# More picked columns on ScalarE, and a new place for the transposes and for the norm's products in a message-passing kernel

## The chip, the cores and the metric

The kernel runs on one core of one Trainium2 chip. The metric is the device time of one execution in microseconds (us); before the change the median of three runs is 3556.44 us. The engines are named as in the profile: PE is TensorE (PEld its weight loads), DVE is VectorE, ACT is ScalarE, POOL is GpSimd, SP issues DMAs; a small q behind a name means the engine's sequencer, which waits and issues.

## The reference

A graph network's layer with 12500 nodes of 128 features (32 scalars and 32 vectors of 3), and 412500 edges that are sorted by the node they point to (`dst`). Each edge has 4 attributes and 8 radial inputs. A residual and a layer norm follow.

```
x0 = x[:, :32];  x1 = x[:, 32:].reshape(N, 32, 3)
feat0, self0 = split(x0 @ W1_0e / sqrt(32));  feat1, self1 = split(einsum('nui,uw->nwi', x1, W1_1o) / sqrt(32))
e0 = feat0[src];  e1 = feat1[src]                        # one row of 128 numbers for each edge
h  = gelu(edge_attr_8 @ W_mlp1 / sqrt(8));  h = gelu(h @ W_mlp2 / sqrt(64))      # 64 wide
w00, w01, w10, w11 = h @ Wp_00, h @ Wp_01, h @ Wp_10, h @ Wp_11                  # 32 wide each
mid0 = [w00 * e0 * ea0,  w11 * sum(e1 * ea1) / sqrt(3)] / sqrt(2)
mid1 = [(w01 * e0) x ea1,  w10 * e1 * ea0] / sqrt(2)
n0, n1 = segment_sum(mid0, dst), segment_sum(mid1, dst)  # over sqrt(32)
y = cos(pi/8) * self + sin(pi/8) * [n0 @ W2_0e, n1 @ W2_1o] / sqrt(64)
out = layernorm(x + y)
```

## The kernel before

**Units of work.** A *run* is 512 edges in 4 columns of 128 (`Q` = 4); there are 806 runs (`NS`). A *chunk* is 4 runs; there are 202 (`NCH`). The main loop has one step per run, `s`; `c` is its chunk and `k` = 0 to 3 its place in the chunk. The order on PE, ACT, DVE and SP is the order in which the code is written; POOL takes its gathers as their operands allow.

**Source rows.** Every edge needs the feature row of its source node, tile `G[s]` of 128 x 4 x 128, in 19 buffers (`LEAD`). `gather(s + 18)` issues one indirect DMA on POOL for each column of the run (L222). The first 18 runs gather from `x` and are multiplied by the weights afterwards (`turn_rows`, `features`); the others gather from a table of features that the prologue computes and stores to memory. Three kinds of column aren't gathered. In every 14th run SP loads one column's 128 rows by single-row DMAs from the table (`aid`, L209). And DVE and ACT each *pick* the nodes of one column out of the transposed input `xT`, which lies in SBUF: each picked node is one copy of a 128 x 1 column to the tile `gt` (L190 on DVE, L192 on ACT), at an address that a register holds. When 128 are together, `picked_rows` multiplies them with the weights (PE, L198), and ACT copies the result into `G` (L199). `SLOTS` says how many columns an engine picks in a run, and in how many register loads (`pick_nodes`) and groups of copies (`pick`): 32 a run on average on DVE, 28 on ACT as 12 and 16. Thus one whole column in every 4 runs is DVE's, and one in every 4.57 runs is ACT's.

**The small network.** In step k = 1 `mlp1` computes the first layer of chunk c + 2 (PE L536, gelu on ACT L540), in step k = 3 `mlp2` the second (PE L551, ACT L556). `radial` turns a chunk's 8 inputs by a PE transpose (L527) and a copy on ACT (L529), for chunk c + 2 in step k = 0. `load_edges` brings them by a DMA from SP four chunks ahead, in step k = 3 (L496). `weights` makes the four products `w` (PE L569). The tiles in PSUM named `h`, which all of these use, have two buffers.

**Messages and sums.** DVE multiplies `w` with `G` to messages `M` in three parts (L637 once, L641 twice a run). `segments` sums them by PE into a window of nodes in PSUM (L666, L668), at places that `tile_places` has computed from the edges' first nodes (`tile_first`, 202 rows of 16 numbers in two tiles). After a chunk DVE adds the window to `acc` (L681).

**Norm.** Nodes are finished in 25 groups of 512. When a group's sums are complete, `norm` runs in the step k = 3 of the chunk after: `moments` multiplies the sums by the output weights (PE L698, L701) and copies the result (ACT L706), `move_sums` moves the rest of `acc` (ACT L428), and DVE clears the free part in quarters, one in each following step k = 1 (L425). `norm_on` (statistics and roots, one step k = 1 later) and `norm_end` (k = 2, scaling on ACT L742, stores from SP L260) follow.

**Other moved parts.** `turn_attributes` turns the 4 attributes of 32 runs (PE L521, ACT L523) and `load_indices` the indices of 128 runs (PE L468).

Of the kernel before, what the change touches and what calls it, by code (L numbers as in the profile page):

```python
# [21 lines left out]
P = 128  # L22
# [3 lines left out]
Q = 4  # L26
# [21 lines left out]
AID_FROM = 22  # L48
AID_LEAD = 16
STEPS = 12  # L50
SLOTS = {DVE: [(12, 12, 0), (12, 12, 8), (12, 12, 8), (12, 12, 16)], ACT: [(12, 16)]}
COL_Q = {DVE: Q - 2, ACT: Q - 3}
COL_FROM = {DVE: 12, ACT: 12}
LNB = 2
TURN_AT = (7, 9, 11, 13, 15, 17, 18, 20, 22, 24)


@with_exitstack
def gnn_kernel(ctx: ExitStack, tc: tile.TileContext, x, src, dst, ea4, ea8, w1_0, w1_1, wm1, wm2,
# [276 lines left out]

    def weight_loads():

        yield w1r, sub(wm1, 0, [[0, P // RAD], [HID, RAD], [1, HID]])
        yield w2b, sub(wm2, 0, [[0, 2], [HID, HID], [1, HID]])  # L340
        for j, w in enumerate((wp00, wp01, wp10, wp11)):
            yield wpb[:, j * MUL:(j + 1) * MUL], sub(w, 0, [[0, 2], [MUL, HID], [1, MUL]])
        for t, w in ((w20, w2_0), (w21, w2_1)):
            yield t[:MUL, :], w[:MUL, :]
            yield t[MUL:, :], sub(w, MUL * MUL, [[0, 3], [MUL, MUL], [1, MUL]])
        yield first_node, sub(dst, 0, [[1, 1], [CH * SB, NCH]])
        for b, t in enumerate(tile_first):
            c0, n = b * P, t.shape[0]
            last = c0 + n == NCH and E < NCH * CH * SB
            if last:  # L350
                yield (t[n - 1:n, :].rearrange("a (k o) -> a k o", o=1),
                       sub(dst, (NCH - 1) * CH * SB, [[1, 1], [0, CH * Q], [1, 1]]))
                k = -(-(E - (NCH - 1) * CH * SB) // P)
                yield t[n - 1:n, :k], sub(dst, (NCH - 1) * CH * SB, [[k * P, 1], [P, k]])
            yield t[:n - last], sub(dst, c0 * CH * SB, [[CH * SB, n - last], [P, CH * Q]])

    def make_w1b():

# [34 lines left out]
    NT = -(-NCH // P)  # L393
    tile_first = [cst.tile([min(P, NCH - b * P), CH * Q], I32, name=f"tf{b}") for b in range(NT)]

    def find_first():

        floor, strays = line(1), line(2)
        steps = [(0, 0)] + [(c + 1, (bs[-1] + 1) * GN) for c, bs in due.items() if c + 1 < NCH]
        for (r, n0), (z, _) in zip(steps, steps[1:] + [(NCH, 0)]):  # L400
            nc.vector.memset(floor[:, r:z], float(n0))
        nc.vector.tensor_tensor(floor, first_node, floor, op=OP.subtract)
        nc.vector.tensor_scalar(strays, floor, 0.0, float(ACC - SPAN), op0=OP.max, op1=OP.min)
        nc.vector.tensor_copy(first_at, strays)
        nc.vector.tensor_tensor(strays, strays, floor, op=OP.not_equal)
        nc.vector.tensor_reduce(odd[0:1, 2 * NB:2 * NB + 1], strays, axis=mybir.AxisListType.X, op=OP.add)

    def tile_places():

        for b, t in enumerate(tile_first):  # L410
# [233 lines left out]

    def places(c):

        b, r = divmod(c, P)
# [34 lines left out]


    pend, done = [], []
    before_last = due[NCH - 1][0] - 1

    def moments(b, sums=None):
        n0, nn, full, tail, tiles = group(b)
        if not pend:
            Y["y"] = wk.tile([P, LNB, XB, P], F32, name="y", bufs=1)  # L690
            Y["v"] = wk.tile([P, LNB * XB, 2], F32, name="mv")
            nc.vector.memset(Y["v"], 1.0)
        j = len(pend)
        pend.append(b)
        pt = ps.tile([P, XB, P], F32, name="h")
        at = n0 - base[-1] if b in due[NCH - 1] else 0
        for t, k in tiles:
            nc.tensor.matmul(pt[:k, t, :], xT[:, n0 + t * P:n0 + t * P + k], ws, start=True, stop=sums is not None)  # L698
            if sums is None:
                for a in range(4):  # L700
                    nc.tensor.matmul(pt[:k, t, :], A["now"][:, a, at + t * P:at + t * P + k], wpost[:, a, :],  # L701
                                     start=False, stop=a == 3)
            else:
                nc.vector.tensor_tensor(pt[:k, t, :], pt[:k, t, :], sums[:k, t, :], op=OP.add)
        if full:
            nc.scalar.activation(Y["y"][:, j, :full, :], pt[:, :full, :], AF.Copy)  # L706
        if tail:
            nc.scalar.activation(Y["y"][:tail, j, full, :], pt[:tail, full, :], AF.Copy)

    def statistics(b):  # L710
        j = pend.index(b)
        st = wk.tile([P, XB, 6], F32, name="bst")
        for t, k in group(b)[4]:
            nc.vector.bn_stats(st[:k, t, :], Y["y"][:k, j, t, :])
            nc.vector.bn_aggr(Y["v"][:k, j * XB + t, :], st[:k, t, :])

    def deviations():
# [5 lines left out]
    def normalise(last=False, keep=False):  # L723
# [9 lines left out]
        for j, b in enumerate(pend):  # L733
            if b in done:
                continue
            for t, k in group(b)[4]:
                i = j * XB + t - i0
                if last and t % 2:
                    nc.vector.tensor_scalar(y[:k, j, t, :], y[:k, j, t, :], r[:k, i:i + 1], m[:k, i:i + 1],
                                            op0=OP.mult, op1=OP.add)  # L740
                    continue
                nc.scalar.activation(y[:k, j, t, :], y[:k, j, t, :], AF.Identity,  # L742
                                     bias=m[:k, i:i + 1], scale=r[:k, i:i + 1])
            store_nodes(nc.sync, out, b, y[:, j])
        done[:] = pend if keep else []
        if not keep:
            pend.clear()

    def norm(bs):
        for b in bs:  # L750
            moments(b)
            move_sums()
            new_sums()

# [11 lines left out]
    def norm_last(bs):  # L766
# [6 lines left out]
        if len(pend) > len(done):  # L773
            deviations()
            normalise(True)

    odd_f = cst.tile([1, 1], F32)
    odd_i = cst.tile([1, 1], I32)
# [117 lines left out]
    with tc.manual_schedule(engines={PE, ACT, DVE, SP}):  # L896
# [7 lines left out]
        for b in range(min(AHEAD, NG)):  # L904
# [9 lines left out]
                 NG // 2 + 9: tile_places, NG // 2 + 10: lambda: mlp2(1), NG // 2 + 11: make_ws, NG: make_wpost}  # L914
        for b in range(NG + 2):
            if b < NG:
                turn(b)
# [28 lines left out]
        for s in range(NCH * CH + CH):  # L946
# [56 lines left out]
            if k < 3 and s < NS:  # L1003
                pick_nodes(DVE, s, 2)
                pick(DVE, P)
            if k == 1 and 1 < c < NCH:
                norm_on(due.get(c - 2, []))
            if k == 2 and 1 < c < NCH - 1:
                norm_end(due.get(c - 2, []))
            if k == 0 and c == NCH:  # L1010
                norm_end(due.get(c - 3, []))
                norm_on(due.get(c - 2, []))
                norm_end(due.get(c - 2, []))
# [53 lines left out]
```

## Time and profile before

| | us |
|---|---|
| median of 3 runs | 3556.44 (3555.64 to 3560.35) |
| the profiled execution | 3556.29 |
| its span, from first to last instruction | 3554.4 |
| PE busy | 3159.9 |
| DVE busy | 3129.2 |
| ACT busy | 2797.6 |
| POOL busy | 2667.6 |

Busy time is that of instructions in the engine; what a sequencer does, such as loading registers or issuing DMAs, isn't in it. In a row of the groups stands: line, engine, operation, output <- inputs, shapes, count, then busy us and mean ns of one, and after the second bar the engine's idle time just before them with what ended it. In a row of waits stands who waited for whom: us in total, times, longest. In a row of the timeline stands the start and the length in us, and in brackets the idle time before. In a row by windows stands the stretch, its length, and then the busy time and count.

### The profile page before, as it was taken

What the parts mean: (1) busy time and instruction counts of PE and PEld (TensorE: products, weight loads), DVE (VectorE), ACT (ScalarE), POOL (GpSimd) and SP (SyncE); (2) the same over time, 40 slices, a digit from 0 to 9 for tenths busy, and PEclk for the clock granted to TensorE, in tenths of its full rate; (3) what the DMA queues carried; (4) which work ended last, traced back from release to release, by engine and by line L of the source; (5) the groups of instructions that cost most, each with busy time, mean ns of one, the idle gap of its engine ahead of it and who ended that gap; (6) DMA issues with size and microseconds to landing.
All of it is one profiled execution on the core that took longest, in us unless ns stands there. A gap on an engine that the chain in (4) does not pass through costs nothing. (4 is left out here: it accounts for less than half of the span.)

```text
span 3554.4 us, 143693 instructions
## 1 busy us (share of the span) xinstructions
PE 3159.9 (89%) x28598; PEld 2755.6 (78%) x28598; DVE 3129.2 (88%) x29317; ACT 2797.6 (79%) x23671; POOL 2667.6 (75%) x2804
## 2 busy tenths in 40 slices
PE   6899898998898988998899898898899989888888
PEld 6777777787777777877788787787787777777777
DVE  2699999999999999999899899888899888889897
ACT  3488788788888888887887888877787887788785
POOL 7777777777777777777777777777777777777775
PEclk8999999998999999899998899989899999999998
DMA  8322332223322223322323323323323232232221
GB/s 199 70 62 68 63 64 65 63 61 74 64 60 67 63 60 74 64 60 62 68 61 70 67 59 64 65 63 68 65 62 64 59 69 63 60 69 63 60 65 47
DMA packets 579225, 239.29 MB, mean 67 GB/s; under 512 B 483651, under 2 KB 528747, under 8 KB 578347
## 3 DMA queue, kind: packets, MB, share of 16 engines
q0 software_dynamic: 89536, 183.55, 20.3%
q1 hardware_dynamic: 468041, 40.02, 9.1%
q10 hardware_dynamic: 20770, 6.47, 0.8%
q8 instruction: 252, 4.13, 0.5%
q14 instruction: 626, 5.13, 0.5%
HBM read 217.00 MB, written 12.80 MB: 65 GB/s over the span
## 5 line engine op out<-in xcount | busy, mean ns | idle before, releaser
L222 POOL DMA_INDIRECT G<-table,idx x2726 | 2598.9, 953 | 836.7 <-issue 718.5
L192 ACT ACTIVATE gt<-xT 128x1 f32 x22016 | 2166.7, 190 | 73.3 <-issue 53.6
L190 DVE COPY gt<-xT 128x1 f32 x25216 | 1728.6, 144 | 212.1 <-issue 172.9
L666 PE MATMUL sums<-own,M 128*128 128x96 f32 x6446 | 1354.8, 294 | 74.3 <-DVE M L641 73.0
L668 PE MATMUL sums<-own,M 128*128 128x96 f32 x6446 | 1319.7, 288 | 85.1 <-DVE M L641 84.1
L666 PEld LDWEIGHTS sums<-own,M 128*128 128x128 f32 x6446 | 1037.5, 201 | 181.9 <-DVE M L641 101.7
L668 PEld LDWEIGHTS sums<-own,M 128*128 128x128 f32 x6446 | 1035.3, 202 | 108.9 <-DVE M L641 107.6
L641 DVE TENSOR_TENSOR M<-w,G 128x384 f32<-128x384 f32 x1612 | 880.1, 547 | 0.0
L569 PE MATMUL w<-wpb,h 64*128 64x128 f32 x6448 | 649.3, 305 | 57.8 <-DVE M L641 56.3
L569 PEld LDWEIGHTS w<-wpb,h 64*128 64x128 f32 x6448 | 496.5, 197 | 199.6 <-issue 74.3
L637 DVE TENSOR_TENSOR M<-w,G 128x256 f32<-128x256 f32 x806 | 333.4, 414 | 34.4 <-issue 19.9
L540 ACT ACTIVATE h<-h 128x512 f32<-128x512 f32 x404 | 216.3, 586 | 178.6 <-PE h L536 165.7
L536 PE MATMUL h<-eT,w1b 64*128 64x128 f32 x3232 | 288.7, 319 | 8.4 <-ACT e L523 8.3
L536 PEld LDWEIGHTS h<-eT,w1b 64*128 64x128 f32 x3232 | 241.3, 218 | 38.7 <-ACT e L523 13.7
L556 ACT ACTIVATE h<-h 128x512 f32<-128x512 f32 x404 | 213.5, 577 | 26.3 <-PE h L551 22.5
L551 PE MATMUL h<-h,w2b 64*64 64x256 f32 x3232 | 222.6, 391 | 0.0
L199 ACT ACTIVATE G<-h 128x128 f32<-128x128 f32 x369 | 96.4, 277 | 120.5 <-PE h L198 76.4
L198 PE MATMUL h<-wf,gt 128*128 128x128 f32 x738 | 143.5, 294 | 1.9 <-ACT h L556 0.9
L529 ACT ACTIVATE eT<-h 128x128 f32<-128x128 f32 x202 | 56.0, 277 | 112.7 <-PE h L527 89.5
L551 PEld LDWEIGHTS h<-h,w2b 64*64 64x64 f32 x3232 | 104.5, 133 | 44.8 <-issue 0.5
L630 DVE TENSOR_TENSOR own<-oh,e 128x512 f32<-128x512 f32 x202 | 137.6, 681 | 0.7 <-issue 0.2
L681 DVE TENSOR_TENSOR acc<-sums,acc 128x384 f32 x202 | 111.2, 550 | 9.7 <-issue 6.2
(113 smaller groups left out, 1329.1 us busy)
## 6 DMA issues: line engine op xcount, KB each, us to landing
G<-table SPq DMA_DIRECT2D x7168, 0.5 KB
G<-table,idx POOLq DMA_INDIRECT x2726
e<-in_edge_attr SPq DMA_DIRECT2D x201, 64.0 KB
own<-in_x SPq DMA_DIRECT2D x24, 256.0 KB
table<-acc ACTq DMA_DIRECT2D x24, 256.0 KB
xt<-in_edge_attr SPq DMA_DIRECT2D x24, 256.0 KB
out<-y SPq DMA_DIRECT2D x24, 256.0 KB
xt<-in_dst SPq DMA_DIRECT2D x5, 256.0 KB
```

The lines of the kernel that those rows point to most:

```text
L190: nc.vector.tensor_copy(to, col)
L192: nc.scalar.activation(to, col, AF.Copy)
L222: nc.gpsimd.indirect_dma_start(out=G[s][:, q, :], out_offset=None, in_=x if s < raw_runs else table, in_offset=bass.IndirectOffsetOnAxis(a ...
L536: nc.tensor.matmul(p1[h][:, j // 2, j % 2, :], w1b[rows, j, :], eT[c][rows, :], start=True, stop=True)
L540: nc.scalar.activation(H1[c][h], p1[h].rearrange("p k j e -> p (k j e)"), AF.Gelu_apprx_tanh, scale=1.0 / math.sqrt(RAD))
L551: nc.tensor.matmul(p2[r][k * HID:(k + 1) * HID, h * n:(h + 1) * n], w2b[rows, :], H1[c][h][rows, k * n:(k + 1) * n], start=True, stop=True)
L556: nc.scalar.activation(H2[c][r].rearrange("p k j e -> p (k j e)"), p2[r], AF.Gelu_apprx_tanh, scale=1.0 / math.sqrt(HID))
L569: nc.tensor.matmul(WP[i][:, q, :], H2[c][q % 2][rows, k, q // 2, :], wpb[rows, :], start=True, stop=True)
L637: nc.vector.tensor_tensor(M[s][:, :, :, :MUL], w[:, :, :2 * MUL].rearrange("p q (a u) -> p q a u", a=2), g[:, :, None, :MUL].to_broadcast( ...
L641: nc.vector.tensor_tensor(M[s][:, :, j, MUL:].rearrange("p q (i u) -> p q i u", i=3), w[:, :, None, (2 + j) * MUL:(3 + j) * MUL].to_broadc ...
L666: nc.tensor.matmul(flat[:, bass.ds(at, 4 * FIRST_HALF)].bitcast(F32), M[s][:, q, 0, :], own[:, 3 * WIDE:], start=False, stop=False)
L668: nc.tensor.matmul(sb[:, 1:, bass.ds(at, 4 * WIDE)].bitcast(F32), M[s][:, q, 1, :], own[:, :3 * WIDE].rearrange("p (a j) -> p a j", a=3), ...
```

## The change

- `SLOTS` of ACT becomes (12, 8, 12): 32 columns a run in three register loads, with a `pick` in every step and a third `pick_nodes` behind it. The loads of the picked nodes' numbers follow from the numbers in `SLOTS`.
- `radial` moves from k = 0 (for chunk c + 2) to k = 2 (for chunk c + 3); `turn_attributes` from step 21 of 32 to step 24, `load_indices` from step 64 of 128 to step 66.
- `norm` is split: `norm_products` in the step k = 0 of the second chunk after the group's last, `norm_keep` (copy, move of the sums, start of the clearing) in k = 1, `norm_on` and `norm_end` at k = 2 and k = 0 after it.
- The group before the last makes the products of three of its four tiles in earlier chunks (`part`); for that `find_first` counts an edge that would still touch those tiles as odd, which leads to a general path. The last group is normalised from PSUM, and each of its tiles is stored by its own DMA, in turn from SP and ACT.
- The table of first nodes comes as tiles of 16, 128 and 58 rows; the first is loaded first in the prologue, the others after the loads of picked nodes, and `tile_places` treats them in step 9.

```diff
-SLOTS = {DVE: [(12, 12, 0), (12, 12, 8), (12, 12, 8), (12, 12, 16)], ACT: [(12, 16)]}
+SLOTS = {DVE: [(12, 12, 0), (12, 12, 8), (12, 12, 8), (12, 12, 16)], ACT: [(12, 8, 12)]}
...
+FIRST_TILES = 16
...
     def weight_loads():
 
+        yield from tile_loads(0)
         yield w1r, sub(wm1, 0, [[0, P // RAD], [HID, RAD], [1, HID]])
...
+    tile_from = [0, *range(FIRST_TILES, NCH, P)]
...
+        for t, (a, z) in enumerate(zip(done_at, done_at[1:])):
+            nc.vector.tensor_scalar(strays[:, a + 1:z + 1], strays[:, a + 1:z + 1], float((t + 1) * P), None, op0=OP.max)
...
-    def moments(b, sums=None):
+    def moments(b, sums=None, part=None, hold=False):
         n0, nn, full, tail, tiles = group(b)
+        if part is not None:
+            tiles = tiles[part:part + 1]
...
+        if sums is None and b == NG - 1:
+            Y["pt"] = pt
+            return
+        if part is not None:
+            nc.scalar.activation(Y["y"][:, j, part, :], pt[:, part, :], AF.Copy)
+            return
+        if hold:
+            Y["held"] = Y["y"][:, j], pt
+            return
...
+                if last:
+                    eng = nc.sync if t % 2 else nc.scalar
+                    eng.dma_start(out[b * GN + t * P:b * GN + t * P + k, :], y[:k, j, t, :])
+            if not last:
+                store_nodes(nc.sync, out, b, y[:, j])
...
+    def norm_products(bs):
+        for b in bs:
+            assert group(b)[3] == 0
+            moments(b, hold=True)
+
+    def norm_keep(bs):
+        for b in bs:
+            y, pt = Y.pop("held")
+            nc.scalar.activation(y, pt, AF.Copy)
             move_sums()
             new_sums()
...
-        late = list(aid_load())
+        late = list(aid_load()) + [load for b in range(1, NT) for load in tile_loads(b)]
...
-            if s % P == P // 2 and (s // P + 1) * P < NS:
+            if s % P == P // 2 + 2 and (s // P + 1) * P < NS:
                 load_indices(s // P + 1)
...
             pick(ACT, P)
+            if k == 1 and 1 < c < NCH - 2:
+                norm_keep(due.get(c - 2, []))
+                clearing += [(c, a) for a in range(4)] if c - 2 in due else []
             pick_nodes(ACT, s, 1)
...
-            if k == 0 and c + 2 < NCH:
-                radial(c + 2)
-            if s % ET == 21 and s - 21 + ET < NS:
+            if s == 0:
+                radial(2)
+            if k == 2 and c + 3 < NCH:
+                radial(c + 3)
+            if s % ET == 24 and s - 24 + ET < NS:
                 turn_attributes(s // ET + 1)
...
+            pick(ACT, P)
+            pick_nodes(ACT, s, 2)
             if k % 2 and c + 2 < NCH:
-                pick(ACT, P)
                 (mlp1 if k == 1 else mlp2)(c + 2)
...
-            if k == 1 and 1 < c < NCH:
+            if k == 2 and 2 < c < NCH - 1:
+                norm_on(due.get(c - 3, []))
+            if k == 0 and 3 < c < NCH - 1:
+                norm_end(due.get(c - 4, []))
+            if k == 1 and c == NCH - 1:
                 norm_on(due.get(c - 2, []))
-            if k == 2 and 1 < c < NCH - 1:
-                norm_end(due.get(c - 2, []))
...
-            if k == (1 if end else 3) and 0 < c < NCH:
+            if k == 0 and 1 < c < NCH - 2:
+                norm_products(due.get(c - 2, []))
+            if k == 1 and c == NCH - 2:
                 norm(due.get(c - 1, []))
-                clearing += [(c, a) for a in range(4)] if c - 1 in due and not end else []
+            if k == 0 and (c - 3 == done_at[0] or c - 2 in done_at[1:-1]):
+                moments(before_last, part=0 if c - 3 == done_at[0] else done_at.index(c - 2))
...
+            if s == 9:
+                tile_places(range(1, NT))
```

More of the change, by code (lines that the diff above doesn't have):

```diff
@@ L346, in weight_loads, with tile_loads @@
         yield first_node, sub(dst, 0, [[1, 1], [CH * SB, NCH]])
[L347 to L355, printed above, removed]
+    def tile_loads(b):
+        t, c0 = tile_first[b], tile_from[b]
+        n = t.shape[0]
+        last = c0 + n == NCH and E < NCH * CH * SB
+        if last:
+            yield (t[n - 1:n, :].rearrange("a (k o) -> a k o", o=1),
+                   sub(dst, (NCH - 1) * CH * SB, [[1, 1], [0, CH * Q], [1, 1]]))
+            k = -(-(E - (NCH - 1) * CH * SB) // P)
+            yield t[n - 1:n, :k], sub(dst, (NCH - 1) * CH * SB, [[k * P, 1], [P, k]])
+        yield t[:n - last], sub(dst, c0 * CH * SB, [[CH * SB, n - last], [P, CH * Q]])
     def make_w1b():
@@ L392, in gnn_kernel @@
     first_at = cst.tile([1, NCH], I32)
-    NT = -(-NCH // P)
-    tile_first = [cst.tile([min(P, NCH - b * P), CH * Q], I32, name=f"tf{b}") for b in range(NT)]
+    tile_from = [0, *range(FIRST_TILES, NCH, P)]
+    NT = len(tile_from)
+    tile_first = [cst.tile([z - a, CH * Q], I32, name=f"tf{b}")
+                  for b, (a, z) in enumerate(zip(tile_from, tile_from[1:] + [NCH]))]
+    before_last = due[NCH - 1][0] - 1
+    assert len(due[NCH - 1]) == 1
+    done_at = [math.ceil((before_last * GN + (t + 1) * P + MARGIN) / N * NCH) - 1 for t in range(XB)]
+    assert due[done_at[-1]] == [before_last] and done_at == sorted(set(done_at))
+    assert not any(c in due for c in (*range(done_at[0] - 1, done_at[-1]), 0, NCH - 4, NCH - 2)) and done_at[-1] < NCH - 2
     def find_first():
@@ L645, in places @@
     def places(c):
-        b, r = divmod(c, P)
+        b = max(b for b, a in enumerate(tile_from) if a <= c)
+        r = c - tile_from[b]
         _, PLACE[c] = nc.values_load_multi_w_load_instructions(
@@ L692, in moments @@
             nc.vector.memset(Y["v"], 1.0)
-        j = len(pend)
-        pend.append(b)
+        if b not in pend:
+            pend.append(b)
+        j = pend.index(b)
         pt = ps.tile([P, XB, P], F32, name="h")
@@ L708, in moments, with rows_of @@
             nc.scalar.activation(Y["y"][:tail, j, full, :], pt[:tail, full, :], AF.Copy)
+    def rows_of(b, j, t, k):
+        return Y["pt"][:k, t, :] if b == NG - 1 and "pt" in Y else Y["y"][:k, j, t, :]
     def statistics(b):
@@ L737, in normalise @@
                 i = j * XB + t - i0
+                z = rows_of(b, j, t, k)
                 if last and t % 2:
-                    nc.vector.tensor_scalar(y[:k, j, t, :], y[:k, j, t, :], r[:k, i:i + 1], m[:k, i:i + 1],
+                    nc.vector.tensor_scalar(y[:k, j, t, :], z, r[:k, i:i + 1], m[:k, i:i + 1],
                                             op0=OP.mult, op1=OP.add)
[L741 to L744, printed above, removed]
+                else:
+                    nc.scalar.activation(y[:k, j, t, :], z, AF.Identity,
+                                         bias=m[:k, i:i + 1], scale=r[:k, i:i + 1])
+                if last:
+                    eng = nc.sync if t % 2 else nc.scalar
+                    eng.dma_start(out[b * GN + t * P:b * GN + t * P + k, :], y[:k, j, t, :])
+            if not last:
+                store_nodes(nc.sync, out, b, y[:, j])
         done[:] = pend if keep else []
@@ L750, in norm @@
         for b in bs:
-            moments(b)
+            moments(b, part=XB - 1 if b == before_last else None)
+            move_sums()
+            new_sums()
+    def norm_products(bs):
[3 more added lines that the diff above has]
+    def norm_keep(bs):
+        for b in bs:
+            y, pt = Y.pop("held")
+            nc.scalar.activation(y, pt, AF.Copy)
             move_sums()
@@ L775, in norm_last @@
             normalise(True)
+        Y.pop("pt")
     odd_f = cst.tile([1, 1], F32)
```

11 lines of the change are left out of this document (4 added, 7 removed).

## The prediction

> **What bounds the kernel now.** I read the page's busy shares and costliest groups first, then busy time by windows, the waits of single engines in two stretches, and the timeline at both ends. No engine looks full, and POOL (GpSimd, which issues the gathers) least of all.
>
> ```profile
> PE 3159.9 (89%) x28598; PEld 2755.6 (78%) x28598; DVE 3129.2 (88%) x29317; ACT 2797.6 (79%) x23671; POOL 2667.6 (75%) x2804
> L222 POOL DMA_INDIRECT G<-table,idx x2726 | 2598.9, 953 | 836.7 <-issue 718.5 <-DVE M L641 50.2 <-DMA G<-table,idx 34.4
> L192 ACT ACTIVATE gt<-xT 128x1 f32 x22016 | 2166.7, 190 | 73.3 <-issue 53.6
> L190 DVE COPY gt<-xT 128x1 f32 x25216 | 1728.6, 144 | 212.1 <-issue 172.9
> ...
> 200.00:2200.00 2000.00, 1800.51 (x16433) 1566.44 (x16434) 1827.97 (x17443) 1642.49 (x14144) 1515.43 (x1590) 0.94 0.30 65
> 2200.00:3500.00 1300.00, 1156.47 (x10356) 1007.59 (x10356) 1160.98 (x11054) 1041.80 (x8923) 984.64 (x1035) 0.92 0.30 64
> ```
>
> The last two rows are busy time by windows, in the order PE, PEld, DVE, ACT, POOL. The gathers (L222) take 2598.9 + 836.7 = 3435.6 us with the idle time before them, 97% of the span, and nearly all of that idle time is a fixed 0.30 us before each. POOL's timeline shows it at the start and at the end: a gather every 1.25 us, and one stop, 5.68 us, before the first gather from the table.
>
> ```profile
> 92.74 0.94 POOL L222 DMA_INDIRECT G<-in_x,idx_raw  x1 [0.30 <-issue]
> 99.37 0.94 POOL L222 DMA_INDIRECT G<-table,idx  x1 [5.68 <-DVE M L641]
> ...
> 3527.07 0.94 POOL L222 DMA_INDIRECT G<-table,idx  x1 [0.30 <-issue]
> 3528.32 0.94 POOL L222 DMA_INDIRECT G<-table,idx  x1 [0.30 <-issue]
> ```
>
> So POOL is saturated from 99 to 3529 us, though the page calls it 75% busy. It starts 18 runs ahead, and the other engines use that lead up. The first product of a run's messages (L637) counts the runs that VectorE has begun; its waits for gathered rows (SEEN, L597) show when the lead is gone.
>
> ```profile
> 0.00:200.00 200.00, 9.94 (x24) 0.93 0.56 126
> 200.00:2200.00 2000.00, 195.38 (x472) 0.94 0.30 65
> 2200.00:3500.00 1300.00, 123.52 (x299) 0.92 0.30 64
> ...
> DVE gt L190 <- issue: 103.1, 291, 0.9
> DVE acc L425 <- ACT acc L428: 14.0, 7, 4.7
> DVE SEEN L597 <- DMA G<-table,idx: 0.6, 1, 0.6
> ...
> DVE SEEN L597 <- DMA G<-table,idx: 36.2, 31, 2.1
> ```
>
> The first three rows are L637 by windows, the next three VectorE's waits from 200 to 2200 us, the last its wait from 2200 to 3500. There are two regimes. Until 2200 us VectorE runs at its own pace, 2000/472 = 4.237 us a run, waiting for little but the issue of its own copies. Afterwards it hangs on POOL: 1300/299 = 4.348 us a run, while 1035 gathers in 1300 us are 1.256 us each, 3.46 a run. ScalarE (ACT) and TensorE have slack in both.
>
> **The change: gathers.** 32 columns a run instead of 28, in some 794 runs, are 3176 more copies on ScalarE and 3176/128 = 25 columns fewer to gather: 2726 becomes 2701. 25 x 1.256 = 31.4 us leave POOL's chain. What is late next is VectorE: the 782 runs after 200 us at 4.237 end in a last run begun at 200 + 3313 = 3513 us, where it now begins at 3538.12 (row below). So of the 31 us about 25 can be had before VectorE's own pace shows.
>
> **ScalarE.** One copy costs 1300.25/13217 = 0.0984 us.
>
> ```profile
> 200.00:2200.00 2000.00, 1300.25 (x13217) 0.94 0.30 65
> 1005.49 4.41 ACT L192 ACTIVATE gt<-xT 128x1 f32 x44
> ...
> ACT h L540 <- PE h L536: 75.9, 55, 5.6
> ACT y L706 <- PE h L701: 63.8, 14, 6.0
> ACT eT L529 <- PE h L527: 59.8, 48, 8.3
> ACT G L199 <- PE h L198: 41.1, 61, 2.8
> ACT gt L192 <- issue: 31.5, 132, 0.6
> ACT e L523 <- PE h L521: 22.7, 11, 4.8
> ```
>
> The first row is L192 by windows, the others ScalarE's timeline and its waits from 200 to 2200 us. The stretch of 44 copies runs at 0.1 us each with register loads inside it and no gap, so I cost the third load at nothing: copies already queued hide it. With that cover gone it is one gap of 0.24 us (31.5/132) in each of 794 runs, 190 us of ScalarE. ScalarE is busy 1642.5/472 = 3.480 us a run and idle 357.5/472 = 0.757. Four more copies make 3.874. It keeps VectorE's 4.237 if its idle time shrinks to 0.363 a run, 48% of what it is. The moves aim there: the norm's products go a step ahead of their copy (y, 63.8), the turned attributes (e, 22.7) and the turned edge data (eT, 59.8) go to steps without a layer: 146 of 357.5 us, 41%. The rest should come by itself: in those waits ScalarE is early, and it now arrives 0.39 us later per run. I take it that ScalarE just keeps pace.
>
> **Added waits.** Clearing the next sums now stands in the same step as ScalarE's move of the old ones (two steps later before), and behind it in VectorE's order wait its picks and the next messages. That wait exists already: 14.0 us in 7 places. Bounds for 24 groups: none, or 4.7 us each (113 us); the mean of the 7, 2.0 us, at half of them is 24 us, against 18.9 us that L425 idles now: I add 5 us.
>
> ```profile
> L425 DVE MEMSET acc<- 128x512 f32 x96 | 46.6, 485 | 18.9 <-ACT acc L428 14.0
> ...
> SPq L260 <- ACT y L742: 180.9, 24, 20.2
> ...
> 1186.07 0.40 SPq L496 DMA_DIRECT2D e<-in_edge_attr  x1
> 1194.49 0.27 PE L527 MATMUL h<-ident,e 128*128 128x128 f32 x1
> 2384.13 2.74 DMA e<-in_edge_attr
> ```
>
> The stores of the normalised rows block SP until ScalarE has made them (second row, 7.5 us each); they move from the step just ahead of the edge load to three steps ahead of it, so SP has longer to catch up: nothing. The edge data is turned two steps (some 10 us) earlier, but its load is issued where it was. The closest pair that I found is in rows three and four, 8.42 us from issue to turning, and one load took 2.74 us (row five, from the chain), so there TensorE would stand some 4 us. TensorE's 10% of idle time hides that, 0 to 4 us if it doesn't; I take 0. The index turning and the register loads of places move with nothing else behind them: 0.
>
> **The start.** Before, about 3200 four-byte elements of the first-node tables go out just ahead of an edge load, whose issue is held 8.94 us; behind it 16 loads of picked nodes take SP 11.40 us, and ScalarE's queue, with its table stores, waits for one of them.
>
> ```profile
> 66.80 8.94 SPq L496 DMA_DIRECT2D e<-in_edge_attr  x1
> 75.78 1.05 SPq L959 DMA_DIRECT2D aid_at<-in_src  x1
> 76.87 11.40 SPq L959 DMA_DIRECT2D pick<-in_src  x16
> ...
> 81.75 1.08 ACT L540 ACTIVATE h<-h 128x512 f32<-128x512 f32 x2 [10.13 <-DMA pick<-in_src]
> ```
>
> Now 256 elements go early and the rest behind the picks' loads, which are 4 and not 16, since 32 divides 128. That takes 0 to 10.1 us off. The elements still go out in the same 20 us, so I take the middle, 5, for both chains (POOL can gain 5.68 at most).
>
> **The end.**
>
> ```profile
> 3527.97 0.41 PE L698 MATMUL h<-ws,xT 128*128 128x128 f32 x2
> 3531.57 1.06 PE L701 MATMUL h<-wpost,acc 128*128 128x128 f32 x8
> ...
> 3536.21 0.42 DVE L637 TENSOR_TENSOR M<-w,G 128x256 f32<-128x256 f32 x1 [5.08 <-PE w L569]
> 3538.12 0.43 DVE L637 TENSOR_TENSOR M<-w,G 128x256 f32<-128x256 f32 x1 [0.55 <-PE sums L668]
> ...
> 3546.44 0.26 ACT L708 ACTIVATE y<-h 84x128 f32<-84x128 f32 x1
> 3549.97 0.72 SPq L262 DMA_DIRECT2D out<-y  x1
> ```
>
> The products of four tiles (3527.97 to 3532.63) hold back the last weights. Three of them go to earlier chunks: 3.5 us of the 5.08 us stall. The last group is normalised where it lies, without the 0.4 us of copies, and each tile is stored at once on two queues, for which I take the 0.72 us issue: 1.2 us in all, 0 to 3 by the rows around it.
>
> **Sum.** VectorE's chain to its last run: 3513 - 5 (start) + 5 (clear) + 1.6 (rest of the stall) = 3514.6. POOL's chain: 3538.1 - 31.4 - 3.5 - 5 = 3498.2. The later one decides. From there 3554.4 - 3538.1 = 16.3, less 1.2, is 15.1: a span of 3529.7. The profiled execution took 3556.29 us, 1.9 over its span and 0.15 below the median of 3556.44, so the forecast is 3532 us, 24 us (0.7%) less.
>
> **Rivals.** *ScalarE becomes the bound (slower).* If its waits stay, because TensorE and ScalarE hold each other up through shared buffers and not because ScalarE is early, it sets the pace. At 65% kept: 3.874 + 0.492 = 4.366 us a run, 200 + 782 x 4.366 + 1.6 + 15.1 = 3631, so 3633 us. If all stay: 4.631 a run, 3840 us. It decides from 48% kept and ends above the time before from 4.268 a run, 52% kept. For it: the margin is that thin, and waits of 8.3 us are longer than the added copies of a step. Against: y, e and eT are a large part, and each has been moved.
>
> *The busiest engines decide (no change).* TensorE and VectorE are busy 89 and 88%. If they set the end all along, gathers taken off POOL give nothing, and only the end moves: 3556.3 - 3.5 - 1.2 = 3551.6 us. Against it stand POOL's unbroken rows and VectorE's change of pace at 2200 us. The Trainium skill argues this way in Perfetto Trace Analysis, section Identifying the Most-Contended Engine: work on the engine with the highest occupancy, which for GpSimd is a fair measure. This trace differs: at 75% occupancy POOL issues a gather every 1.25 us without a break.
>
> *Both chains improve fully (faster still).* With 10 us at the start and no wait at the clear (-19), VectorE is at 3486 and POOL decides: 3538.1 - 31.4 - 3.5 - 5.7 = 3497.5, plus 15.1 and 1.9, 3515 us.
>
> **How the numbers follow.** The forecast, from 3515 to 3549 us, has 0.64, the better case 0.06: faster 0.70. The busiest engines deciding has 0.05, ScalarE at its break-even 0.05: same 0.10. ScalarE as the bound has 0.20: slower. A measurement of this kernel can tell about 0.2%, 7 us, from no change. The range goes from 3512, just below POOL's limit, to 3572, ScalarE at 4.288 a run (55% kept); the dearer part of that rival and little else stays outside.
>
> **What would show it.** Right: 2701 table gathers, still 1.25 us apart; 25216 copies on ScalarE; y and e nearly gone from its waits and its busy share near 88%; no wait of VectorE for gathered rows after 2200 us; the last wait for w below 2 us. Wrong: ScalarE without idle time while TensorE or VectorE wait for L540, L556 or L428; gaps over 0.3 us on POOL, waiting for buffers that VectorE has not freed; L425 waiting over 24 us; table stores still held near 81 us.

## The result and the profile after

The changed kernel takes 3675.01 us (median of 4 runs, 3661.53 to 3681.86) against 3557.41 us (4 runs, 3555.64 to 3560.35) before: a ratio of 1.0332, with a 95% interval from 1.0309 to 1.0354. It is 118 us slower where 24 us less was forecast, and it lies above the range. The profiled execution took 3674.5 us, its span 3672.7 us, and the granted TensorE clock was 0.902 over the span.

The page of the changed kernel first: busy shares and the two groups that were forecast. Lines have moved: the gathers are L223 now (L222 before), ScalarE's picks L193 (L192), VectorE's first product L653 (L637), the transpose of the edge data L543 with its copy L545 (L527, L529), the picked columns' products L199 with their copy L200 (L198, L199), the clear L441 (L425).

```profile
PE 3225.9 (88%) x28648; PEld 2793.7 (76%) x28648; DVE 3131.9 (85%) x29244; ACT 3117.9 (85%) x26897; POOL 2642.5 (72%) x2779
L223 POOL DMA_INDIRECT G<-table,idx x2701 | 2573.6, 953 | 923.0 <-issue 744.4
L193 ACT ACTIVATE gt<-xT 128x1 f32 x25216 | 2467.7, 191 | 30.6 <-issue 20.8
```

The counts are as forecast: 2701 gathers and 25216 copies. But every engine has a smaller busy share than before save ScalarE, and POOL's idle time before the gathers grew from 836.7 to 923.0 us although there are 25 fewer. POOL no longer decides. The groups of TensorE and then the waits of TensorE, ScalarE and VectorE show who does. In a row of waits stand the waiting instruction, what ended the wait, the sum in us, how many, and the longest.

```profile
L683 PE MATMUL sums<-own,M 128*128 128x96 f32 x6446 | 1388.0, 300 | 4.4 <-DVE M L657 4.3
L685 PE MATMUL sums<-own,M 128*128 128x96 f32 x6446 | 1350.9, 294 | 6.6 <-DVE M L657 6.5
L585 PE MATMUL w<-wpb,h 64*128 64x128 f32 x6448 | 601.7, 307 | 2.8 <-DVE M L657 2.8
...
PE h L199 <- ACT eT L545: 305.4, 183, 3.0
...
ACT h L572 <- PE h L567: 195.0, 108, 3.4
ACT G L200 <- PE h L199: 85.4, 183, 1.6
...
DVE acc L441 <- ACT acc L444: 141.9, 23, 8.1
```

TensorE waits 305.4 us in 183 places, 1.67 us each. Its next largest wait comes to 38.8 us (the transpose L543, for the copy L556), and its waits for VectorE's messages ahead of L683, L685 and L585 are 4.3 + 6.5 + 2.8 = 13.6 us. The large wait stands ahead of the picked columns' products and is for ScalarE's copy of the turned edge data, whose values those products do not read. The timeline of one such place, ScalarE first and then TensorE, tells why.

```profile
1009.62 1.08 ACT L556 ACTIVATE h<-h 128x512 f32<-128x512 f32 x2 [0.17 <-ACT gt L193]
1010.59 2.32 ACT L193 ACTIVATE gt<-xT 128x1 f32 x24
1012.81 0.26 ACT L545 ACTIVATE eT<-h 128x128 f32<-128x128 f32 x1
1013.12 0.28 ACT L200 ACTIVATE G<-h 128x128 f32<-128x128 f32 x1
1013.65 0.28 ACT L200 ACTIVATE G<-h 128x128 f32<-128x128 f32 x1 [0.25 <-PE h L199]
...
1011.12 0.27 PE L543 MATMUL h<-ident,e 128*128 128x128 f32 x1
1011.23 0.39 PE L199 MATMUL h<-wf,gt 128*128 128x128 f32 x2
1013.12 0.49 PE L199 MATMUL h<-wf,gt 128*128 128x128 f32 x2 [1.51 <-ACT eT L545]
1013.54 0.71 PE L585 MATMUL w<-wpb,h 64*128 64x128 f32 x8
```

In one step with k = 2 TensorE writes three tiles named `h`: the transpose at 1011.12, the first picked column's product at 1011.23, the second's at 1013.12. There are two buffers. The third tile needs the buffer of the first, and that is free when ScalarE has copied `eT`, at 1012.81 to 1013.07. ScalarE is late with it because 24 picks, 2.32 us, stand ahead of the copy in its queue. Behind the third tile on TensorE's queue wait the products `w` (L585) and all the sums. The Trainium skill, in Perfetto Trace Analysis, section Optimization Strategy under Identifying Performance Opportunities, says that the same gap repeating on the engine that should be full can mean too little room in SBUF or PSUM for the next tile; this trace agrees, with 183 gaps.

Why two picked columns fall together is in the numbers: 32 divides 128, so ScalarE completes a column in every 4th run, as VectorE does, and the two always meet. Counted from the records, both products follow the transpose within 3.5 us in 194 of 202 chunks; before the change one product followed it in 98 chunks, and never two.

### The profile page after: what moved, and what is told of

Read it like the earlier page. It is cut to its first block, busy times and chain, and to the rows that moved or that the text cites. A ratio compares the mean times of both kernels' runs of the same rounds, so it can differ in the third digit from the quotient of the medians.

```text
span 3672.7 us, 147140 instructions
## 1 busy us (share of the span) xinstructions
PE 3225.9 (88%) x28648; PEld 2793.7 (76%) x28648; DVE 3131.9 (85%) x29244; ACT 3117.9 (85%) x26897; POOL 2642.5 (72%) x2779
## 4 chain that ended last, share of the span: by engine, by line
ACT 37%; PE 29%; DVE 13%; issue 7%; SPq 4%; ACTq 3%; DMA 2%; POOL 2%; DVEq 2%; POOLq 0%
ACT gt L193 28%; PE sums L683 7%; DVE gt L191 7%; PE sums L685 6%; PE h L567 4%; PE w L585 4%; DVE M L657 3%; ACT h L572 3%; SPq L210 3%; ACTq L179 3%; ACT h L556 2%; PE h L199 2%; PE h L720 2%; POOL G L223 2%; DVEq L179 1%
## 5 line engine op out<-in xcount | busy, mean ns | idle before, releaser
L223 POOL DMA_INDIRECT G<-table,idx x2701 | 2573.6, 953 | 923.0 <-issue 744.4
L193 ACT ACTIVATE gt<-xT 128x1 f32 x25216 | 2467.7, 191 | 30.6 <-issue 20.8
L683 PE MATMUL sums<-own,M 128*128 128x96 f32 x6446 | 1388.0, 300 | 4.4 <-DVE M L657 4.3
L685 PE MATMUL sums<-own,M 128*128 128x96 f32 x6446 | 1350.9, 294 | 6.6 <-DVE M L657 6.5
L683 PEld LDWEIGHTS sums<-own,M 128*128 128x128 f32 x6446 | 1083.9, 208 | 89.8 <-issue 14.9
L685 PEld LDWEIGHTS sums<-own,M 128*128 128x128 f32 x6446 | 1078.6, 210 | 8.9 <-DVE M L657 8.7
L585 PE MATMUL w<-wpb,h 64*128 64x128 f32 x6448 | 601.7, 307 | 2.8 <-DVE M L657 2.8
L585 PEld LDWEIGHTS w<-wpb,h 64*128 64x128 f32 x6448 | 460.0, 200 | 149.7 <-issue 106.8
L199 PE MATMUL h<-wf,gt 128*128 128x128 f32 x788 | 199.7, 339 | 325.0 <-ACT eT L545 305.4
L199 PEld LDWEIGHTS h<-wf,gt 128*128 128x128 f32 x788 | 128.7, 206 | 381.9 <-ACT eT L545 342.7
L572 ACT ACTIVATE h<-h 128x512 f32<-128x512 f32 x404 | 219.3, 595 | 206.8 <-PE h L567 195.0
L653 DVE TENSOR_TENSOR M<-w,G 128x256 f32<-128x256 f32 x806 | 334.5, 415 | 67.8 <-PE w L585 37.0
L556 ACT ACTIVATE h<-h 128x512 f32<-128x512 f32 x404 | 219.3, 595 | 96.5 <-PE h L552 58.7
L567 PE MATMUL h<-h,w2b 64*64 64x256 f32 x3232 | 292.2, 491 | 0.0
L552 PE MATMUL h<-eT,w1b 64*128 64x128 f32 x3232 | 236.6, 286 | 0.0
L552 PEld LDWEIGHTS h<-eT,w1b 64*128 64x128 f32 x3232 | 197.8, 189 | 19.1 <-ACT gt L193 0.2
L200 ACT ACTIVATE G<-h 128x128 f32<-128x128 f32 x394 | 107.0, 272 | 92.5 <-PE h L199 85.4
L441 DVE MEMSET acc<- 128x512 f32 x96 | 46.6, 485 | 146.0 <-ACT acc L444 141.9
```

Source lines behind the costliest of these rows:

```text
L193: nc.scalar.activation(to, col, AF.Copy)
L199: nc.tensor.matmul(pt, GT.pop((e, i)), wf, start=True, stop=True)
L223: nc.gpsimd.indirect_dma_start(out=G[s][:, q, :], out_offset=None, in_=x if s < raw_runs else table, in_offset=bass.IndirectOffsetOnAxis(a ...
L552: nc.tensor.matmul(p1[h][:, j // 2, j % 2, :], w1b[rows, j, :], eT[c][rows, :], start=True, stop=True)
L567: nc.tensor.matmul(p2[r][k * HID:(k + 1) * HID, h * n:(h + 1) * n], w2b[rows, :], H1[c][h][rows, k * n:(k + 1) * n], start=True, stop=True)
L572: nc.scalar.activation(H2[c][r].rearrange("p k j e -> p (k j e)"), p2[r], AF.Gelu_apprx_tanh, scale=1.0 / math.sqrt(HID))
```

## The experiments

**Theory A**: the clear holds VectorE (141.9 us), and the rest follows. **Theory B**: the third tile in two buffers holds TensorE. **Theory C**: four more copies a run are more than ScalarE can carry, wherever they stand. e1 to e4 ran on one chip, e5, e6, b1 and b2 on another, b3 and b4 later on that one. The ratio of each is to runs of the kernel before on its own chip, so across these groups the ratios compare better than the times.

### The clearing begun later (e1)

```
             if k == 1 and 1 < c < NCH - 2:
                 norm_keep(due.get(c - 2, []))
-                clearing += [(c, a) for a in range(4)] if c - 2 in due else []
...
             if k == 1 and clearing and c < NCH:
                 clear_sums(clearing.pop(0)[1])
+            if k == 1 and 1 < c < NCH - 2:
+                clearing += [(c, a) for a in range(4)] if c - 2 in due else []
```

> The changed kernel with the clearing of the next sums begun one chunk later (its first quarter in the next step k = 1 and not in the step of ScalarE's move). Theory A (VectorE's wait at the clear is the loss: 141.9 us in 23 places, 6.2 us each, in a chunk that takes 22.9 us where the kernel before took 20.3): L441's wait falls below 20 us and the time by 60 to 140 us, to 3535 to 3615. Theory B (TensorE stands for the third tile in two buffers, 305 us for eT before L199): the time falls by less than 30 us. Theory C (ScalarE's added copies set the pace as such): the wait moves to another place on VectorE, most likely the add of the next sums, and the time falls by less than 30 us.

Measured: 3682.19 us, ratio 1.0353 (1.0336 to 1.037). The waits of TensorE and VectorE:

```profile
PE h L199 <- ACT eT L545: 301.4, 180, 2.1
...
DVE M L653 <- PE w L585: 150.6, 86, 6.0
```

The clear's wait is gone, and VectorE waits as long for TensorE's products `w` instead (37.0 us in the changed kernel). The time did not fall, so the 141.9 us were time that VectorE would have lost to a late TensorE anyway. Theory A falls.

### One tile for both columns (e2)

```
-    def picked_rows(e, i):
-
-        pt = ps.tile([P, P], F32, name="h")
-        nc.tensor.matmul(pt, GT.pop((e, i)), wf, start=True, stop=True)
-        nc.scalar.activation(G[picked[e][i]][:, COL_Q[e], :], pt, AF.Copy)
+    def picked_rows(made):
+
+        pt = ps.tile([P, len(made), P], F32, name="h")
+        for n, (e, i) in enumerate(made):
+            nc.tensor.matmul(pt[:, n, :], GT.pop((e, i)), wf, start=True, stop=True)
+        for n, (e, i) in enumerate(made):
+            nc.scalar.activation(G[picked[e][i]][:, COL_Q[e], :], pt[:, n, :], AF.Copy)
...
```

> The changed kernel with the products of both picked columns (L199) in one tile of PSUM instead of two, so that the step k = 2 takes two tiles named h, not three. Theory B: TensorE's wait for eT (305 us) is gone and the time falls by 60 us or more, to 3615 or less. Theory A: the wait is gone, but the time falls by less than 40 us, since the norm's chunks keep their length. Theory C: less than 15 us, the wait goes into TensorE's other waits for ScalarE.

Measured: 3522.02 us, ratio 0.9895 (0.9878 to 0.9911), 153 us under the changed kernel (155 by the ratios) with the same number of instructions on every engine. Below are the timeline of TensorE at the same place of a chunk, the waits of TensorE and VectorE, POOL's group, and its first and last gather from the table. Lines stand two further on.

```profile
1019.24 0.27 PE L545 MATMUL h<-ident,e 128*128 128x128 f32 x1
1019.35 0.61 PE L200 MATMUL h<-wf,gt 128*128 128x128 f32 x4
1019.88 0.71 PE L587 MATMUL w<-wpb,h 64*128 64x128 f32 x8
...
PE sums L687 <- DVE M L659: 81.3, 116, 1.0
PE sums L685 <- DVE M L659: 64.8, 89, 2.5
PE w L587 <- DVE M L659: 63.1, 65, 2.7
...
DVE acc L443 <- ACT acc L446: 27.7, 17, 4.5
DVE SEEN L615 <- DMA G<-table,idx: 20.4, 20, 2.0
...
L225 POOL DMA_INDIRECT G<-table,idx x2701 | 2578.2, 955 | 824.0 <-issue 704.7 <-DMA G<-table,idx 56.4 <-DVE M L659 36.0
...
94.06 0.94 POOL L225 DMA_INDIRECT G<-table,idx  x1 [0.30 <-issue]
...
3495.02 0.95 POOL L225 DMA_INDIRECT G<-table,idx  x1 [0.31 <-issue]
```

Both products run in one piece behind the transpose, and `w` follows at once. Theory B is shown. TensorE's 305.4 us for `eT` don't all come back, since now it waits for VectorE again: 81.3 + 64.8 + 63.1 = 209.2 us instead of 13.6. 305.4 less 195.6 is 110 us, and TensorE's busy time is 40 us less (3225.9 against 3185.6); together 150 of the 153 us. The clear's wait falls to 27.7 us without being touched, and POOL's idle time is 0.305 us a gather again.

### Both edits (e3), and one copy for both columns (e6)

e3 is e2 with the clearing begun later. e6 is e3 with one ScalarE copy for both columns, which lie side by side:

```
+        if len(made) == 2:
+            (e, i), (f, j) = made
...
+            nc.scalar.activation(G[picked[e][i]][:, COL_Q[e]:COL_Q[f] + 1, :], pt, AF.Copy)
+            return
...
```

> Both edits together. Theories A and B together: POOL becomes the bound again, 2701 gathers 1.25 us apart, 3515 to 3535 us. A alone: as the later clearing. B alone: as the one tile. C: above 3640.

> The changed kernel with one PSUM tile for both picked columns, the clearing begun one chunk later, and one ScalarE copy of 128x256 for both columns where there were two of 128x128; the two columns lie side by side for that. Saves about 0.2 us of ScalarE's work in each of 197 groups, some 40 us of its busy time. If ScalarE still sets part of the pace with one tile: 3495 to 3512 us. If POOL's gathers decide, 2701 x 1.25 us, as they should with one tile: 3512 to 3522 us, no change against the version with two copies (3519 us).

Measured: 3518.84 us for e3, ratio 0.9896 (0.988 to 0.9913), and 3521.96 us for e6, ratio 0.9893 (0.9877 to 0.991). Neither differs from e2. Beyond the third tile the clear has nothing left to give here. On ScalarE's work e6 says little: it was to take 40 us off ScalarE's busy time, but took 7 (3093.2 us in e3, 3086.3 in e6). In e2 the 2701 gathers go from 94.06 to 3495.02 us, 1.26 us each, so POOL is the floor again.

### ScalarE's columns back to 28 (e4)

```
-SLOTS = {...  ACT: [(12, 8, 12)]}
+SLOTS = {...  ACT: [(12, 16)]}
```

> The changed kernel with ScalarE back at 28 columns in two loads (12, 16); the moved steps, the start and the end stay. Theory C: the loss is gone, 3530 to 3560 us (gathers as before, start and end better). Theory A: ScalarE is less late at the move, but the clear still follows it within the step: the wait at L441 stays above 50 us and the time is 3570 to 3620. Theory B: with ScalarE's columns at other runs there are fewer steps with three tiles; 3560 to 3600.

Measured: 3547.65 us, ratio 0.9973 (0.9964 to 0.9983). The page's busy shares and TensorE's wait:

```profile
PE 3186.9 (90%) x28598; PEld 2780.3 (78%) x28598; DVE 3134.1 (88%) x29326; ACT 2812.4 (79%) x23672; POOL 2671.3 (75%) x2804
...
PE h L199 <- ACT eT L545: 15.7, 24, 1.5
```

With the edge data still turned at k = 2, the wait is nearly gone. Counted as above, both products follow the transpose in 73 chunks now, one alone in 122. By itself this does not tell B from C, since it takes away the copies too; and of 73 places only 24 wait, so that ScalarE's shorter queue has a part in it. It does price the columns: from here to e2, which besides the one tile differs by the columns alone, the main loop makes 25 gathers fewer, and the time falls by 25.6 us (the one tile, which takes away the 15.7 us of waits, may have a part in it).

### The edge data turned at k = 0 again (e5)

```
-            if s == 0:
-                radial(2)
-            if k == 2 and c + 3 < NCH:
-                radial(c + 3)
+            if k == 0 and c + 2 < NCH:
+                radial(c + 2)
```

> The changed kernel with one move undone: the edge data is turned again in the step with k=0 for chunk c+2, so that the step with k=2 makes two tiles named h and not three; 32 columns and all else stay. Theory B (three tiles in two buffers in one step): TensorE's wait for ScalarE's copy of eT ahead of L199 falls from 305 us to under 20, and the time to 3515 to 3550 us. Theory C (four more copies a run set ScalarE's pace, whatever step they stand in): the time stays above 3640 us. Theory A (the clear): 3660 to 3680 us, since the clear stands where it stood.

Measured: 3522.07 us, ratio 0.9896 (0.9879 to 0.9912). The longest of TensorE's waits at L199:

```profile
PE h L199 <- ACT h L556: 30.7, 24, 3.4
```

The wait for `eT` is gone from them, and the time is that of e2, with 25216 copies and two tiles for the columns. Theory C falls: the copies fit into this order of the steps. One moved call of the change costs 153 us (155 by the ratios).

### Parts of the change put on the kernel before (b1 to b4)

b1 has only the 32 columns, b2 only the start and the end, b3 both, and b4 is b1 with the edge data turned at k = 2:

```
b1: -SLOTS = {...  ACT: [(12, 16)]}
    +SLOTS = {...  ACT: [(12, 8, 12)]}
    ...
    +            pick(ACT, P)
    +            pick_nodes(ACT, s, 2)
                 if k % 2 and c + 2 < NCH:
    -                pick(ACT, P)
b2: the change's first-node tiles, late loads, parts of the group before last and the last group's stores
b4: b1, and
    -            if k == 0 and c + 2 < NCH:
    -                radial(c + 2)
    +            if s == 0:
    +                radial(2)
    +            if k == 2 and c + 3 < NCH:
    +                radial(c + 3)
```

> The kernel before with the 32 columns alone: three loads a run, 3176 more copies on ScalarE and 25 gathers fewer; the turned edge data stays at k=0, and the norm, the clear and the ends stay as before. Theory B: the copies themselves fit into ScalarE's idle time, both picked columns fall into k=2 without a third tile there, and the time is 3525 to 3548 us. Theory C: ScalarE at 4.37 us a run or more, 3630 us or above. By the prediction's sum for the columns alone, without its 5 us at the start and 4.7 us at the end: 3540 us.

> The kernel before with the start and the end of the change alone: 256 elements of the first-node tables early and the rest late, parts of the group before last done in earlier chunks, the last group normalised where it lies, its tiles stored on two queues. ScalarE keeps 28 columns, and the gathers stay 2726. By the prediction's terms 5 + 3.5 + 1.2 = 9.7 us are saved: 3547 us. If the 12.3 us by which the first messages came earlier in the changed kernel are worth as much at the end: 3540 us. If POOL's 2726 gathers can't start earlier, and only the end counts: 3552 us.

> The start and the end of the change with the 32 columns, on the kernel before: the norm's products and copies, the clear, the attributes, the indices and the edge data stay in the steps of before. If the norm's moves are what makes the four columns worth anything: about 10 us under the columns alone, 3545 to 3552 us. If the start or the end is what the columns lack: 3515 to 3527 us, as with the moves.

> The kernel before with the 32 columns and the edge data turned in the step with k=2, and nothing else of the change: three tiles named h in that step, two buffers, no move of the norm or of the clear. Theory B (the third tile): over 100 us above the columns alone (3560 us), 3660 to 3720 us, and TensorE waits some 250 to 330 us for ScalarE's copy of eT ahead of L198. If the moved norm or clear has a part in the loss: 3570 to 3640 us.

| | columns | start, end | norm and other moves | edge data at | us | ratio (95%) |
|---|---|---|---|---|---|---|
| b2 | 28 | new | old | k = 0 | 3550.20 | 0.9973 (0.9963 to 0.9983) |
| e4 | 28 | new | new | k = 2 | 3547.65 | 0.9973 (0.9964 to 0.9983) |
| b1 | 32 | old | old | k = 0 | 3559.82 | 0.9989 (0.9973 to 1.0005) |
| b3 | 32 | new | old | k = 0 | 3537.74 | 0.9941 (0.992 to 0.9961) |
| e5 | 32 | new | new | k = 0 | 3522.07 | 0.9896 (0.9879 to 0.9912) |
| after | 32 | new | new | k = 2 | 3675.01 | 1.0332 (1.0309 to 1.0354) |
| b4 | 32 | old | old | k = 2 | 3750.10 | 1.0527 (1.0496 to 1.0558) |

b4 is the counter-test: the third tile alone, with nothing of the norm or the clear moved, costs 190 us on b1 (3559.82 to 3750.10). TensorE's wait in it:

```profile
PE h L198 <- ACT eT L529: 302.6, 178, 2.9
```

It is the wait of the changed kernel. That kernel, with everything else in it, is some 69 us faster than b4 by the ratios, so the rest of the change helps.

b1 missed: 3525 to 3548 us was expected by theory B and 3540 by the prediction's sum, and 3559.82 came, no change from before by its interval. Its runs lie far apart (3542.14 to 3567.77). b3 lies between what its two cases expected; the start and end bring 17 us to the columns by the ratios, and the moves another 16 (0.9941 to 0.9896). The intervals of b1, b3 and e5 don't overlap, but each of the two steps can be some 9 us more or less by them. With 28 columns the same moves bring nothing (b2 to e4, though e4 turns the edge data at k = 2). The rows by windows from 200 to 2200 us show where the engines stand. First b1, b3 and e2, all engines (stretch, length, then busy PE, PEld, DVE, ACT, POOL), then VectorE's first product in b1, b3 and e2:

```profile
200.00:2200.00 2000.00, 1794.69 (x16296) 1562.12 (x16296) 1805.03 (x17191) 1803.64 (x15877) 1511.89 (x1581) 0.93 0.29 64
200.00:2200.00 2000.00, 1799.15 (x16402) 1563.29 (x16402) 1816.51 (x17293) 1814.47 (x15976) 1515.38 (x1587) 0.94 0.29 64
200.00:2200.00 2000.00, 1831.08 (x16506) 1597.20 (x16504) 1827.92 (x17455) 1825.50 (x16092) 1515.52 (x1589) 0.92 0.29 65
...
200.00:2200.00 2000.00, 193.09 (x466) 0.93 0.29 64
200.00:2200.00 2000.00, 194.78 (x470) 0.94 0.29 64
200.00:2200.00 2000.00, 196.48 (x475) 0.92 0.29 65
```

b1 begins 466 runs, 4.292 us each, where the kernel before has 472 and e2 475 (4.211). ScalarE is idle (2000 - 1803.64)/466 = 0.421 us a run in b1, 0.395 in b3 and 0.367 in e2. POOL does not decide in b1: its last gather from the table goes out at 3518.92 us, and VectorE begins its last run 26.8 us later, where it was 9.8 us before the change and 7.6 in e2. So what the 25 gathers release is spent on VectorE's side. That this comes from ScalarE's waits in the old steps fits the three rows, but it is argued and not shown: there is one profile of each kernel, that of b1 is of one of its longer executions (3565.4 us), and b1 and b3 differ in these rows though only the start and the end set them apart. Which of the moves it is (norm, attributes or indices) was not separated either.

## Why the prediction was wrong

**The step that failed** is "The rest should come by itself", together with "The edge data is turned two steps (some 10 us) earlier [...] I take 0". Turning the edge data at k = 2 was costed by its load alone, and it was counted as a gain for ScalarE, since `eT` leaves the step of a layer. What was not asked is which tiles share its two buffers in the new step. 32 columns put both picked products there every 4th run, and the third tile makes TensorE stand 305.4 us for a copy that ScalarE reaches only behind its picks; that wait was taken as 0. In the fences of the prediction eT stood as something ScalarE waits for; the move turned it into something TensorE waits for.

**The rival had it.** "TensorE and ScalarE hold each other up through shared buffers" is the mechanism, with 0.20; it was set by a share of kept waits rather than by naming the tile. ScalarE waits in its turn for what TensorE makes late: 195.0 us ahead of the second layer's L572, where it was 22.5 before. The windows of the changed kernel, all engines and then VectorE's first product:

```profile
200.00:2200.00 2000.00, 1765.36 (x15648) 1525.03 (x15648) 1738.12 (x16515) 1744.15 (x15247) 1470.00 (x1543) 0.90 0.29 63
200.00:2200.00 2000.00, 185.94 (x448) 0.90 0.29 63
```

ScalarE is busy 1744.15/448 = 3.893 us a run (3.874 forecast) and idle 255.85/448 = 0.571, 75% of the 0.757 of before, against the 65% that the rival was worked out with. Busy and idle time add up to the pace, 4.464 us, by the way they are counted, so that is no test of the rival's sum; fed with this pace the sum gives 200 + 782 x 4.464 + 1.6 + 15.1 = 3707.5 us, 35 above the span, since 26 runs and not 24 are begun by 200 us and the pace after 2200 us is better, 1300/295 = 4.407. e2 keeps 0.367, 48.5%, where the forecast needed 48%. The forecast described a kernel with two tiles in that step.

**The signs.** Several signs named for being right came, while the time rose: the waits for y and e are nearly gone (7.9 + 2.3 and 0.2 us; 111.9 and 52.0 before), VectorE waits 1.4 us for gathered rows after 2200 us, and the last wait for w is under 2 us. The gathers' spacing, 1.29 us on average with the idle time, and ScalarE's busy share, 85%, spoke against. The list for being wrong named waits for L540, L556 and L428, but not for the copy of `eT` (L529), which was the one.

**ScalarE's third load**, costed at nothing, holds: its waits for issue are 20.8 us ahead of the picks, fewer than the 53.6 before, and 18.0 in e2, where ScalarE is not held up by TensorE's stall.

**Gathers.** 31.4 us off POOL's chain is confirmed once the wait is gone: e2's last gather is issued at 3495.02, 31.7 us before that of e4 (3526.73) and 33.3 before that of the kernel before (36.4 by the 31.4 and the 5 at the start). That the time from e4 to e2 falls by 25.6 us, near the 25 taken as usable, is in part luck: VectorE's own pace was to cap the gain, but in e2 POOL is the floor, and 2.9 of the 31.7 us go behind the last gather: from there to the last run it takes 7.6 us, and to the end of the span 17.5 more, in e4 6.2 and 16.0. The profiled execution of e4 is also 3.1 us above its median. In the changed kernel the gain is lost under TensorE's wait.

**VectorE's own pace** was taken as 4.237 us a run; e2's 4.211 is a little faster.

**The clear** was costed at 5 us, with bounds to 113. It reads 141.9 us in the changed kernel, but 27.7 in e2 and, moved away, gives nothing: a symptom, as e1 showed. L425 waiting over 24 us had been named as a sign of error, and was one, though not of its own cause.

**Start and end.** From the timeline of the changed kernel: VectorE's first message, POOL's first gather from the table, the last two runs of VectorE.

```profile
86.07 0.42 DVE L653 TENSOR_TENSOR M<-w,G 128x256 f32<-128x256 f32 x1
93.97 0.94 POOL L223 DMA_INDIRECT G<-table,idx  x1 [0.30 <-issue]
...
3653.52 0.42 DVE L653 TENSOR_TENSOR M<-w,G 128x256 f32<-128x256 f32 x1 [1.97 <-PE w L585]
3655.43 0.42 DVE L653 TENSOR_TENSOR M<-w,G 128x256 f32<-128x256 f32 x1 [0.55 <-PE sums L685]
```

The first message comes 12.3 us earlier (98.40 before), above the bound of 10.1, and POOL's first table gather 5.4 us earlier, its stop of 5.68 gone. The last wait for `w` is 1.97 us, 3.1 of the 3.5 us forecast and just under the 2 us named. From the last run to the end of the span it takes 17.3 us, not 15.1 (16.3 before, and 16.3 in b2): the storing of single tiles from PSUM gave no 1.2 us. Together, start and end are worth 9.6 us by b2's ratio (6.0 to 13.2 by its interval), against 9.7 forecast. That the two meet is luck in the parts: in b2's profile the last gather goes out 2.5 us earlier and not 5 (3525.80, 3528.32 before), the last run follows it 3.5 us sooner, as forecast, and the last 1.2 us don't come.

**The busiest engine.** This rival would have given 3551.6 us. In e4 TensorE and VectorE are the busiest too, and POOL shows 75%, yet taking 25 gathers from POOL and adding copies to ScalarE moved the end by 25.6 us. In the changed kernel TensorE's 88% is the highest share, and TensorE is what stands; but its matmuls hardly grew in number (28598 to 28648), so the share does not tell why. The section that the prediction names for this rival (the Trainium skill, Perfetto Trace Analysis, Identifying the Most-Contended Engine) does not take TensorE's matmul share for a good measure and looks, among others, at its weight loads, 76% here; by it VectorE and ScalarE, 85% each, would come first, and this trace, where TensorE's wait decides, differs.

## What to carry to other kernels

Before a step is moved, list the tiles that every piece of its new step takes from a shared pool, in order, and compare the count with the buffers: one tile too many makes the producing engine wait for a consumer whose queue has nothing to do with it. A change of a ratio (28 to 32 columns) also changes which events fall together, so work out the schedule for a full period. And when several waits grow at once, look first at one that names a buffer and not data: the others, here the clear, can be its echo.

## What the runs showed of the hardware

The granted TensorE clock was lower in the kernels with the regular stalls: 0.902 and 0.901 in the changed kernel and e1, 0.895 in b4, but 0.923 to 0.937 in the eight others. With the same 28648 matmuls, TensorE was busy 3225.9 us in the changed kernel and 3185.6 in e2 (clock 0.924), which is some 40 of the 153 us lost. That the clock makes these 40 us is not shown: the picked columns' products alone, behind the stalls, show 199.7 us (L199) against 133.0 (L200 in e2), and some other groups show less. The Trainium skill (TensorE: Matmul & The Clock Gate, Part 1) ties the clock to how busy TensorE has lately been and speaks of idle windows of about 3.4 us; here the added waits for `eT` are 1.67 us on average and 3.0 us at most, so the trace agrees in direction and not in that size. Whether the pauses lower the clock, or the order of the work does, was not tested.
